# Two-layer decoder on one core: tokens loaded a second time in turned form, keys laid out by GpSimd, and a new written order

## The chip, the cores and the metric

The kernel runs on one core of a Trainium2 chip. The metric is device time in microseconds (us) of one execution, with all inputs in device memory at its start and the output there at its end. Before the change, three runs took 1685.7, 1693.88 and 1693.98 us; the median is 1693.88 us.

A core has these engines, each with an instruction queue of its own that is worked off in order: TensorE (PE: matrix products and transposes), VectorE (DVE), ScalarE (ACT), GpSimd (POOL) and SyncE (SP), which here only issues transfers (DMAs). Sixteen DMA engines move the data.

## The reference

What is computed, with 16 sequences of 256 tokens of 128 features, and 64 context rows of 96 features for each sequence:

```python
# layer 0
x = ln(x + attn0(x))                    # 16 heads of 8, causal, scale 1/sqrt(8)
x = ln(x + cross0(x, ctx))              # 8 heads of 16 over the 64 context rows
scores = softmax(x @ gate_w.T)
idx = top_k(scores + gate_b, 6)         # 64 experts, at most 64 tokens each
y = sum(scores[idx] * expert[idx](x))   # silu(x w1) * (x w3), then w2; 88 wide
z = (silu(x @ ws1.T) * (x @ ws3.T)) @ ws2.T
x = ln(x + y + z)
# layer 1
x = ln(x + attn1(x))                    # 16 heads of 64, causal
x = ln(x + cross1(x, ctx))              # 16 heads of 64 over the context rows
x = ln(x + ffn1(x))                     # layer norm, width-limited q, k, v, 8 heads of 16
```

The first attention of layer 0, whose beginning the change touches, computes q, k, v = x @ Wqkv.T, then dots = (q . k) * 8 ** -0.5 per head.

## The kernel before, in words

**Tiling.** A "batch" is one sequence: 256 tokens, which are two tiles of 128 partitions. The kernel goes through these phases:

- Layer 0 up to the routing, for batches 0 to 15: `layer0(b)`, lines 798 to 922. With it runs `contexts` (lines 768 to 782), work that belongs to layer 1: for eight pairs of heads it multiplies the context with the key and query weights (k1x, g1x) and with the value and output weights (v1x, h1x) and writes the products to device memory (gd, hd), from where layer 1 loads them. Each copy out of PSUM goes to a buffer of the tag "fold", of which there are four.
- Shared feed-forward (`shared`: sh, hs, z), groups 0 to 3 of 8.
- Experts, eight groups of eight (`expert_tokens` loads xe from xb, `expert_turned` transposes it, `expert_hidden`, `expert_out`).
- Shared feed-forward, groups 4 to 7.
- Layer 1, `layer1(b)`, lines 1099 to 1231, for batches 0 to 15. It begins by gathering the expert outputs of a batch (ge, from yb), adds them up on VectorE (xr), and goes on with layer norm, transposes and qk.

**One batch of layer 0.** The tokens x are loaded by SyncE (line 799) and transposed on TensorE into PSUM (tp_x), which VectorE copies to xT (`transposed`, lines 298 to 303). Two matmuls give queries and keys in one PSUM bank (qk). VectorE copies the queries and multiplies them by 8 ** -0.5 (qT, lines 809 to 810). The keys are laid out four times, each copy with other heads set to zero, so that four heads can be multiplied side by side on TensorE: `expanded` (lines 648 to 655) makes kx with two operations on VectorE and two on ScalarE, each of which multiplies by one column of the mask sm8. Scores s_0a, softmax (nm, p, ri, rx), transposes of the probabilities (ptp, pT), values (o_0a) and projection (pj_0a) follow, then the layer norm, whose power of -0.5 (rs) GpSimd computes. The residual with its bias (xpb) is also GpSimd's. The cross attention (names with 0x) has the same form; its keys kx0x are laid out by one GpSimd multiplication with broadcast operands.

Then comes the routing. The gate's logits (lg) are followed by a softmax on ScalarE and VectorE and the choice of six experts (chosen). The matmuls "pos" count how many tokens an expert already has; `run` holds the count of the batches before, and VectorE updates it with two additions (lines 890 to 892). From pos VectorE makes the slot numbers. For each of the 2 x 6 choices of a batch VectorE picks the weight (hit) and GpSimd issues an indirect DMA that writes 128 token rows into their slots in xb (192 scatters over the 16 batches). Each scatter waits for the "hit" of its own number. Slots that stay empty must be zero: `clear_slots` (lines 688 to 694) writes 4096 rows of 512 bytes of zeros into xb, and one row into yb, by SyncE's queue; it is recorded as the first part of `contexts`.

**What sets the order.** The instructions of layer 0 and of layer 1 are first recorded, not emitted: a `Recorder` keeps one list of units for each program (the contexts or one batch) and engine. `interleaved` then emits them in the order of a string, where one character stands for one program and one engine:

```python
    for c in order:
        b, e = divmod(LETTERS.index(c), len(ENGINES))
        for trace in waiting[b][e].pop(0):
            trace()
```

ORDER0 holds the order of layer 0 with the contexts, ORDER1 that of layer 1. Within `manual_schedule` the order on TensorE, VectorE, ScalarE and GpSimd stays as emitted; SyncE's transfers may be moved by the scheduler. There are four such stretches in the kernel before: layer 0, the experts, bv with l1_bout, and layer 1. Because the recorder's line 141 makes every call, all rows of the profile show L141, and operations are told apart by the names of their tiles.

**Start.** Loads go by SyncE in the order of the code: context, shared weights (ws1, ws3, ws2), then the weights of layer 0 (lines 656 to 676); the tokens of batch 0 follow in ORDER0. GpSimd builds the masks and sets vx0 and va0 to zero.

**Between experts and layer 1.** Two tiles vaf are set to zero by GpSimd (lines 1088 to 1089). bv is a broadcast copy on VectorE, eight matmuls multiply it with l1_wout (bv_out), and VectorE adds the result to l1_bout (lines 1091 to 1097). l1_bout is read by xpb_1a of batch 0. On VectorE the gathered sums (xr) of batch 0, as they were scheduled, lie between the last operations of the shared feed-forward (hs and the addition of z) and this copy.

## Time and profile before

| | |
|---|---|
| median of three runs | 1693.88 us |
| the profiled execution | 1679.19 us |
| its span (first to last instruction) | 1677.4 us |
| mean granted TensorE clock | 0.959 |
| TensorE busy | 1496.5 us (89%), 12738 matmuls |
| VectorE busy | 1244.2 us (74%), 3788 instructions |
| ScalarE busy | 1108.6 us (66%), 3811 instructions |
| GpSimd busy | 830.6 us (50%), 910 instructions |
| moved by DMA | 73.89 MB, 44 GB/s |
| layer 0, first pos of batch 0 / 8 / 15 | 86.4 / 364.1 / 602.0 us |
| first qk of layer 1 | 711.9 us |

The profile is one execution taken by the hardware profiler. A row of its groups of operations reads: line, engine, operation, names out<-in, shape out<-in, count, then the busy time in us and the mean of one in ns, then the idle time of the engine just before such rows and what ended that idle time. "Busy" does not say "bound": an engine can be busy beside the one that decides, and a stage of the kernel can be bound by another engine than the span as a whole. So shares are read stage by stage here. PEclk is the clock that TensorE was granted in a window, as a share of its full speed[...]. A row in order of time reads: start in us, duration in us, engine, line, operation, names, shapes; in square brackets stands the idle time of that engine before it and who ended it.

### The profile page before, as it was taken

How to read it: one execution, taken by the hardware profiler on the slowest of the kernel's cores; microseconds unless marked ns; L12 is line 12 of the kernel's file. 1: busy time of each engine (PE TensorE's matmuls, PEld its weight loads, DVE VectorE, ACT ScalarE, POOL GpSimd, SP SyncE). 2: the span in 40 equal slices, each digit the busy share in tenths (PEclk: the TensorE clock that was granted, in tenths of full speed). 3: DMA queues.
4: the chain of work that ended last, by engine and by line, in shares of the span. 5: the costliest groups of instructions: out<-in, count | busy, mean ns of one | idle time of the engine just before them, and what ended most of it. 6: DMA issues, size and time to landing. Idle time of an engine off the chain costs nothing.

```text
span 1677.4 us, 36931 instructions
## 1 busy us (share of the span) xinstructions
PE 1496.5 (89%) x12738; PEld 1080.5 (64%) x12738; DVE 1244.2 (74%) x3788; ACT 1108.6 (66%) x3811; POOL 830.6 (50%) x910
## 2 busy tenths in 40 slices
PE   7989988889987679688998999998999999999996
PEld 4655555556554338466776877686777677777774
DVE  5788888879887643355778878777786787788675
ACT  4776777757776312155576777677676767786766
POOL 2144445444435440456727656664564576564441
PEclk9999999989999778789999999999999999999999
DMA  4111111111100066474202233222322333220000
GB/s 142 60 41 34 60 32 33 42 48 55 47 13 1 1 172 190 52 105 48 23 14 34 40 41 44 23 36 14 48 41 31 30 43 42 36 23 4 5 1 11
DMA packets 117190, 73.89 MB, mean 44 GB/s; under 512 B 46555, under 2 KB 106808, under 8 KB 116877
## 3 DMA queue, kind: packets, MB, share of 16 engines
q1 hardware_dynamic: 104717, 58.55, 12.8%
q0 software_dynamic: 12288, 13.00, 10.6%
q8 instruction: 102, 1.67, 0.4%
q14 instruction: 83, 0.68, 0.1%
HBM read 48.05 MB, written 35.65 MB: 50 GB/s over the span
## 4 chain that ended last, share of the span: by engine, by line
PE 52%; DVE 24%; ACT 11%; issue 6%; POOL 4%; DMA 2%; another core or an unknown queue 1%; SPq 0%; POOLq 0%; DVEq 0%; ACTq 0%
PE s_1a L141 5%; PE qk L141 4%; PE o_1a L141 4%; ACT p_0a L141 4%; PE ptp_1a L141 3%; PE s_0a L141 3%; PE ptp_1f L141 3%; PE vp L141 3%; PE pj_1x L141 3%; PE pj_1a L141 2%; PE ptp_0a L141 2%; DVE nm_0a L141 2%; PE s_1x L141 2%; ACT p_1a L141 2%; DVE x L141 2%
## 5 line engine op out<-in xcount | busy, mean ns | idle before, releaser
L141 POOL DMA_INDIRECT xb<-x,slots x192 | 189.1, 985 | 263.9 <-DVE hit L141 212.6
L141 POOL TENSOR_TENSOR p_1a<-p_1a,ri_1a 128x512 f32<-128x512 f32 x192 | 197.3, 1039 | 104.5 <-DVE ri_1a L141 89.3
L141 ACT ACTIVATE p_1a<-s_1a,nm_1a 128x256 f32<-128x256 f32 (+1 forms) x512 | 210.9, 445 | 50.5 <-DVE nm_1a L141 41.7
L141 ACT ACTIVATE p_0a<-s_0a,nm_0a 128x256 f32<-128x256 f32 (+1 forms) x512 | 211.5, 451 | 35.2 <-DVE nm_0a L141 33.6
L141 POOL DMA_INDIRECT ge<-yb,slots x192 | 195.7, 1019 | 54.4 <-issue 51.9
L141 ACT COPY pT_1a<-ptp_1a 128x512 f32<-128x512 f32 x192 | 106.1, 618 | 63.1 <-PE ptp_1a L141 55.1
L141 DVE TENSOR_REDUCE nm_1a<-s_1a 128x2 f32<-128x512 f32 (+1 forms) x192 | 126.1, 673 | 21.4 <-PE s_1a L141 21.3
L141 DVE TENSOR_REDUCE nm_0a<-s_0a 128x2 f32<-128x512 f32 (+1 forms) x192 | 125.0, 682 | 11.8 <-PE s_0a L141 10.5
L141 PE MATMUL qk<-x3T,l_wqkv 128*128 128x256 f32 x512 | 126.9, 390 | 2.7 <-issue 1.4
L141 ACT ACTIVATE p_1f<-s_1f,nm_1f 128x256 f32<-128x256 f32 x256 | 119.0, 499 | 10.4 <-DVE nm_1f L141 9.3
L141 PE MATMUL ptp_0a<-ident,p_0a 128*128 128x128 f32 x768 | 112.1, 281 | 13.5 <-ACT p_0a L141 7.9
L141 ACT COPY pT_0a<-ptp_0a 128x512 f32<-128x512 f32 x192 | 106.4, 615 | 23.7 <-PE ptp_0a L141 18.6
L141 ACT ACTIVATION_READ_ACCUMULATOR p_0a<-s_0a,nm_0a 128x1 f32 x512 | 120.8, 236 | 0.0
L141 ACT ACTIVATION_READ_ACCUMULATOR p_1a<-s_1a,nm_1a 128x1 f32 x512 | 117.9, 230 | 0.0
L141 PEld LDWEIGHTS qk<-x3T,l_wqkv 128*128 128x128 f32 x512 | 95.8, 197 | 20.1 <-issue 7.7
L141 PEld LDWEIGHTS ptp_0a<-ident,p_0a 128*128 128x128 f32 x768 | 86.4, 143 | 34.0 <-ACT p_0a L141 20.6
L141 PE MATMUL ptp_1a<-ident,p_1a 128*128 128x128 f32 x768 | 101.1, 275 | 7.7 <-POOL p_1a L141 3.9
L141 PE MATMUL s_1a<-kT,qT 64*128 64x256 f32 (+1 forms) x1024 | 104.4, 342 | 3.3 <-issue 2.3
L141 POOL TENSOR_TENSOR p_1x<-p_1x,cri_1x 128x512 f32<-128x512 f32 x64 | 65.9, 1044 | 66.6 <-DVE cri_1x L141 41.9
L141 PE MATMUL o_1a<-pT_1a,v 128*64 128x128 f32 x1536 | 95.4, 276 | 3.0 <-ACT p_1a L141 1.2
L141 PEld LDWEIGHTS s_1a<-kT,qT 64*128 64x128 f32 x1024 | 81.5, 192 | 23.3 <-issue 11.4
L141 DVE SCALAR_TENSOR_TENSOR xr<-ge,slot_w,xr 128x128 f32<-128x128 f32 x160 | 61.2, 383 | 46.8 <-DMA ge<-yb,slots 42.7
(258 smaller groups left out, 3710.9 us busy)
## 6 DMA issues: line engine op xcount, KB each, us to landing
gd<-g1x_sb SPq DMA_DIRECT2D x32, 256.0 KB
hd<-h1x_sb SPq DMA_DIRECT2D x32, 256.0 KB
gx<-gd SPq DMA_DIRECT2D x16, 512.0 KB
hx<-hd SPq DMA_DIRECT2D x32, 256.0 KB
xb<-x,slots POOLq DMA_INDIRECT x192
ge<-yb,slots POOLq DMA_INDIRECT x192
e<-in_w1T SPq DMA_DIRECT2D x8, 352.0 KB
e<-in_w3T SPq DMA_DIRECT2D x8, 352.0 KB
```

The source lines that it names most:

```text
L141: r = f(*[made(x) for x in a], **{n: made(x) for n, x in k.items()})
```

## The change

- The tokens are handed over in a second, transposed copy in device memory (xT). `tokens(b)` loads both forms, with three buffers each; the two transposes on TensorE and VectorE's copy of a batch go away.
- At the start SyncE first issues the tokens of batch 0 and wqkv, then the context and the weights of the context keys and values, then the others; the shared weights come last.
- The zero fill of xb and yb is issued from ScalarE's queue, ahead of ScalarE's other work.
- The factor 8 ** -0.5 is multiplied once into the query columns of wqkv, on VectorE (128x128).
- Queries and keys leave PSUM in one ScalarE copy of 128x512 (qkT, two buffers). The four-fold layout of the keys, kx, is one GpSimd multiplication of 128x1024 with two broadcast operands.
- The two additions for `run` move from VectorE to GpSimd.
- vaf is set to zero by VectorE instead of GpSimd.
- There is one `manual_schedule` for all that follows the start. With it the VectorE order before layer 1 is that of the code: hs and z of the last shared groups, vaf, bv and l1_bout come ahead of all xr.
- ORDER0 is another string, with 2492 units instead of 2542. The matmuls of the contexts 1 to 7, which lay in the first 80% of layer 0's TensorE order, now lie in its last 61%; three and a half contexts come after pos of batch 13, and the last of them entirely after pos of batch 15, ahead of the shared feed-forward. ORDER1 keeps the order on TensorE and ScalarE; on VectorE some ten neighbours change places, on GpSimd one rs and two gathers, on SyncE two transfers.

```diff
@@ -32,66 +32,65 @@
 ORDER0 = (
-    ',\'#\'#$#$+$(#)($()*#*))$(*)*)()*))*())*)()*(*()*#*$#*#$**($**(#*)#$%(\'\'$%()\'\')(()*()*(1*)0-#.*((*-**.-(*..(*)#*'
...
+    '\'(16;(*#)+*)#*$#$+$()()*))*())*)()*(*()*#*$#*#$**($**(#*)#(())(()*$*(*$(()*)-*(*-*2.*((*)7**2*(3/40/4.3/74(80@'
...
 ORDER1 = (
...
@@ -654,25 +653,43 @@
-    ctxT = load("ctxT", [DC, B, KV], pool=xt_pool)
     fw = pool_of(phase_ab, name="fw", bufs=2)
-    ws1 = load("ws1T", [D, 2 * INTER], pool=xt_pool)
...
+        def tokens(b):
+
+            x = x0_pool.tile([P, 2, D], F32, tag="xin", bufs=3, name=f"x_{b}")
+            xT = x0_pool.tile([P, T], F32, tag="xinT", bufs=3, name=f"xT_{b}")
+            nc.sync.dma_start(xT, a["xT"][:, b * T : (b + 1) * T])
+            nc.sync.dma_start(x, a["x"][b * T : (b + 1) * T, :].rearrange("(i p) d -> p i d", p=P))
+            return x, xT
+
+        tokens0 = tokens(0)
         l0_wqkv = load("l0_wqkvT", [D, 3 * D], pool=x0_pool)
+
+        nc.scalar.dma_start(
+            xb.rearrange("(s p) d -> p s d", p=P),
+            zero.unsqueeze(1).to_broadcast([P, NSLOT // P, D]),
+        )
+        nc.scalar.dma_start(yb[NSLOT : NSLOT + 1, :], zero[0:1, :])
+
+        nc.vector.tensor_scalar(l0_wqkv[:, :D], l0_wqkv[:, :D], float(8**-0.5), None, ALU.mult)
+        ctxT = load("ctxT", [DC, B, KV], pool=xt_pool)
...
@@ -684,14 +701,6 @@
-        def clear_slots():
...
@@ -797,19 +805,18 @@
-            xT = w2.tile([P, T], F32, tag="xT", name=f"xT_{b}")
-            transposed(x, xT, f"x_{b}")
+            x, xT = tokens(b) if b else tokens0
...
-            qT = w2.tile([P, 1, T], F32, tag="qT0", name=f"qT0_{b}")
-            nc.vector.tensor_scalar(qT[:, 0, :], qk[:, :T], float(8**-0.5), None, ALU.mult)
+            qkT = x0_pool.tile([P, 2, T], F32, tag="qkT0", bufs=2, name=f"qkT0_{b}")
+            nc.scalar.copy(qkT.rearrange("p i t -> p (i t)"), qk)
             kx = kx_pool.tile([P, 4, T], F32, tag="kx0", name=f"kx0_{b}")
-            expanded(qk[:, T:], sm8, kx)
+            nc.gpsimd.tensor_tensor(
+                kx, qkT[:, 1, :].unsqueeze(1).to_broadcast([P, 4, T]), sm8.unsqueeze(2).to_broadcast([P, 4, T]), ALU.mult,
+            )
...
@@ -887,9 +894,9 @@
-            nc.vector.tensor_tensor(run, chosen[:, 0, :], chosen[:, 1, :], ALU.add)
+            nc.gpsimd.tensor_tensor(run, chosen[:, 0, :], chosen[:, 1, :], ALU.add)
             if run_before is not None:
-                nc.vector.tensor_tensor(run, run_before, run, ALU.add)
+                nc.gpsimd.tensor_tensor(run, run_before, run, ALU.add)
...
@@ -921,8 +928,8 @@
-        with tc.manual_schedule(engines=MANUAL):
-            interleaved(rec, [contexts] + [partial(layer0, b) for b in range(B)], ORDER0)
+        ctx.enter_context(tc.manual_schedule(engines=MANUAL))
+        interleaved(rec, [contexts] + [partial(layer0, b) for b in range(B)], ORDER0)
...
@@ -1086,15 +1092,14 @@
     for t in vaf:
-        nc.gpsimd.memset(t, 0.0)
+        nc.vector.memset(t, 0.0)
...
-    with tc.manual_schedule(engines=MANUAL):
-        nc.vector.tensor_copy(bv, l1_bqkv[:, 16:24].unsqueeze(2).to_broadcast([P, 8, P]))
...
+    nc.vector.tensor_copy(bv, l1_bqkv[:, 16:24].unsqueeze(2).to_broadcast([P, 8, P]))
...
@@ -1244,6 +1248,7 @@
         "x": g["x"].reshape(B * T, D),
+        "xT": g["x"].reshape(B * T, D).T,
```

## The prediction

> **What bounds the kernel now.** I read the chain that ended last, then busy time per stage, then the groups by shape, then single engines in order of time. The chain says which engine to watch:
>
> ```profile
> PE 52%; DVE 24%; ACT 11%; issue 6%; POOL 4%; DMA 2%; another core or an unknown queue 1%; SPq 0%; POOLq 0%; DVEq 0%; ACTq 0%
> ```
>
> Half of the span hangs on TensorE, a quarter on VectorE. The stages say where: window, its length, busy time (instructions) per engine, granted clock, DMA share.
>
> ```profile
> core 0: us, PE busy (x) PEld busy (x) DVE busy (x) ACT busy (x) POOL busy (x), PEclk, DMA share, GB/s
> 0.00:20.00 20.00, 12.80 (x66) 8.51 (x66) 7.85 (x28) 2.23 (x4) 9.47 (x30) 1.00 0.74 208
> ...
> 86.40:158.70 72.30, 64.46 (x549) 40.35 (x548) 61.16 (x220) 51.76 (x193) 34.00 (x37) 0.98 0.12 38
> ...
> 295.90:364.10 68.20, 58.54 (x539) 37.00 (x540) 56.69 (x207) 46.83 (x173) 30.76 (x33) 1.00 0.14 43
> ...
> 540.00:602.00 62.00, 33.27 (x245) 19.01 (x246) 40.08 (x164) 20.38 (x63) 26.03 (x28) 0.71 0.02 2
> ...
> 602.00:630.00 28.00, 25.62 (x103) 13.67 (x104) 11.79 (x51) 4.53 (x8) 14.57 (x15) 0.85 0.92 265
> ...
> 675.00:712.00 37.00, 24.24 (x107) 16.65 (x105) 13.30 (x32) 3.64 (x7) 18.12 (x20) 0.73 0.43 55
> ...
> 742.00:1677.00 935.00, 872.62 (x7638) 681.17 (x7636) 711.25 (x1940) 666.25 (x2214) 535.87 (x575) 0.98 0.23 29
> ```
>
> Layer 1 (742 to 1677) is 935 us long and TensorE is busy for 872.6 of them, 93%. The middle of layer 0 (two of its stretches shown) runs at 89% on TensorE and 85% on VectorE: nearly balanced. Two windows hold idle TensorE: the end of layer 0 (540 to 602, 33 of 62 us, clock 0.71) and the start of layer 1 (675 to 712, 24 of 37). I measure layer 0 by the first "pos" matmul of each batch: batch 0 at 86.4 us, batch 12 at 503.2, batch 15 at 602.0, about 35 us a batch.
>
> Prices from the groups by shape (busy sum, mean ns after the bar):
>
> ```profile
> L141 DVE TENSOR_SCALAR kx<-qk,sm 128x256 f32<-128x256 f32 x28 | 13.2, 476 | 2.9 <-ACT kx L141 2.5 <-issue 0.4
> ...
> L141 ACT ACTIVATE kx<-qk,sm 128x256 f32<-128x256 f32 x28 | 12.1, 481 | 13.5 <-DVE kx L141 8.6 <-PE qk L141 3.0 <-issue 1.8
> ...
> L141 POOL TENSOR_TENSOR kx0x<-kT0x,hm 128x512 f32<-128x512 f32 x13 | 13.6, 1048 | 0.0
> ```
>
> and from VectorE's order in time (start, duration):
>
> ```profile
> 303.41 0.41 DVE L141 COPY xT<-tp_x 128x256 f32<-128x256 f32 x1
> ...
> 307.04 0.42 DVE L141 TENSOR_SCALAR qT<-qk 128x256 f32<-128x256 f32 x1 [0.63 <-ACT kx L141]
> ...
> 324.48 0.18 DVE L141 TENSOR_TENSOR run<-chosen 128x64 bf16<-128x64 bf16 x1
> ...
> 301.35 0.23 DVE L141 COPY rx_0a<-ri_0a 128x128 f32<-128x128 f32 x1
> ...
> 332.19 1.37 DVE L141 COPY rx_0a<-ri_0a 128x128 f32<-128x128 f32 x1
> ```
>
> The last row is the same kind of copy as the one before it, but took 1.37 us instead of 0.23. GpSimd's row at that time is
>
> ```profile
> 332.43 1.04 POOL L141 TENSOR_TENSOR kx0x<-kT0x,hm 128x512 f32<-128x512 f32 x1
> ```
>
> so the copy ended with the GpSimd multiply. From 70 to 530 us, each VectorE operation that overlaps a GpSimd elementwise one, against the median of its kind: 66 such GpSimd operations, 52.7 us long, added 14.0 us to VectorE (27%), and the 13 kx0x rows (13.6 us) alone 5.6 (41%).
>
> **The change part by part.**
>
> *Tokens loaded turned, scale folded, one eviction, run on GpSimd.* Each batch loses on VectorE the copy xT (0.42), qT (0.42), two kx (0.95) and two run additions (0.37): 2.16 us, times 16 = 34.6 us. ScalarE loses two kx (0.96) and gains one 128x512 copy (0.61, as pT): 0.35 x 16, about 5 us less. TensorE loses the pair tp_x, 0.4 to 0.7 us, about 0.5 x 16 = 8 us. The second token load is 128 KB per batch while the DMA share is 0.12 to 0.14 and it is issued batches ahead: nothing; uncovered, one load of about 2 us a batch.
>
> *Keys on GpSimd.* No 128x1024 row exists. From 128x256 (0.74) to 128x512 (1.048) a straight line gives 1.66 us, doubling the latter gives 2.10; I take 2.08, as the kx0x row has the same two operands with a broadcast. That is 33 us of GpSimd in all, plus 31 run additions at 0.5 to 0.72 (128x2 and 128x256 rows are 0.72 and 0.74), near 19. GpSimd was busy 0.45 of the middle; 52 us more over 530 is 0.55, no bound by itself. But the Trainium skill ("SBUF — State Buffer", section "Who interferes with whom") speaks against the change: VectorE and GpSimd share a port pair under an exclusive lock, and a VectorE operation with two SBUF inputs or in a fast mode waits for the whole GpSimd instruction. Taken fully, 33 us of kx would stall VectorE for 33 us and eat the 34.6. The rows above say that only 27 to 41% of GpSimd time comes back as delay, because operations from PSUM and gaps fall under it too: 9 to 14 us for kx, 5 for run. I take 16; 14 to 40 goes into the range. VectorE nets 34.6 - 16 = 18.6 us less. On the latency of one batch: qk then went through 0.42 + 4 x 0.48 on two engines, now 0.61 + 2.08, about 1 us later; 27 to 83 TensorE rows lie between qk and the first s_0a in the new order (some 10 us), which cover it. Behind kx on GpSimd wait xpb, rs and scatters; ahead of it may stand a scatter that waits for "hit".
>
> *Zero fill and load order at the start.*
>
> ```profile
> 8.32 5.53 SPq L141 DMA_DIRECT2D yb<-zero  x1
> ...
> 19.94 1.14 PE L141 MATMUL s_0a<-kx,qT 32*128 32x512 f32 x8
> ```
>
> The 2 MB fill of xb sits on SyncE's queue and the first s_0a runs at 19.94 us. After, tokens and wqkv go first, and the fill goes to ScalarE's queue. Against a fill that is out of the way: the skill's page "DMA: Bandwidth & Descriptors", section "Issuing engines are not separate DMA queues", says that transfers issued from another engine share the same 16 DMA engines. The DMA share of the first 20 us, 0.74, and its 4096 rows of zero agree with a shared resource. By the order alone s_0a could come at 12; with shared engines, ScalarE's first copy behind the issue and GpSimd's masks (until about 9) ahead of kx, I estimate 16. Against these 4 us, 32 v0x matmuls, about 2 us of filler, come later. Net -2, between -6 and +3.
>
> *The new order of layer 0.* After removing 8 us, TensorE has 510 - 8 = 502 us up to the last pos; the order also puts the last context (67 us / 7 = 9.6 each) behind it, so 492. The other contexts move from the first 80% of layer 0 to 39 to 100% of it; 2.5 of them (24 us, less 5 for token work that moved too, so 19) now fill the end of layer 0. I build the time of the last pos: 16 us of start with 10 busy; an end window of 62 us now holding 33 + 19 = 52; and 492 - 10 - 52 = 430 between them at the same 0.893, 482 us. Sum 560, against 602: -42. By VectorE alone (478 - 18.6, same shares) it would be 548, so TensorE decides. If the middle falls to 0.87 from waits on GpSimd, +13; if the end only takes half of its filler, +8. The clock was at half for 7, 14 and 20 us of the end window; if a fuller TensorE avoids this, 10 more, kept for the range.
>
> *The last context ahead of the shared feed-forward.* It is 9.6 us of matmuls, but with four buffers for its evictions and its writes to memory. Between 602 and 630 TensorE was busy for 25.6 of 28 us, so nothing absorbs it: 10 to 19, I take +14. The gathers of expert tokens had to wait for the last scatter (620.2) and were done at 629.8; shifting with the end of layer 0 they stay covered. The expert weights' loads interleave with the context's writes; they wait for layer 0's buffers as before, 0.
>
> *Start of layer 1.*
>
> ```profile
> 699.96 0.80 PE L141 MATMUL z<-ws2T,hs 88*128 88x128 f32 x2 [7.14 <-DVE hs L141]
> ...
> 711.92 9.16 PE L141 MATMUL qk<-x3T,l_wqkv 128*128 128x256 f32 x32 [0.61 <-DVE x3T L141]
> ```
>
> ```profile
> 674.53 0.99 POOL L141 MEMSET vaf<- 128x512 f32 x2 [53.32 <-PE yp L141]
> ...
> 711.29 0.72 POOL L141 TENSOR_TENSOR xpb_1a<-x,l_bout 128x256 f32<-128x256 f32 x1 [5.02 <-DVE l_bout L141]
> ```
>
> z waits 7.14 us for hs, whose VectorE operations stood ready from about 688 but behind xr operations that waited for gathers; xpb_1a waits 5.02 for l_bout for the same reason. The change puts the last hs, bv and l_bout ahead of all xr and moves vaf's memsets (0.99 each) to VectorE, where they fall in idle time (13.3 busy of 37). With l_bout early, qk of layer 1 follows the gathers (last landed 698.3), rs (700.3), norm and transposes: about 705.3 instead of 711.9. -6, between -8 and 0. Uncovered, the memsets cost 2.
>
> *Experts and layer 1.* TensorE's order from the first shared matmul to the end is the same row by row; VectorE differs by neighbour swaps. 0, with ±2.
>
> Sum: -42 (which contains the -2 of the start) + 14 - 6 = -34. The profiled execution is 1679.2 us with a span of 1677.4; the after one should be about 1645 with a span of 1643. The median before is 1693.9, 15 us above it (lowest 1685.7); the same difference on the median gives 1660.
>
> **The rivals.** What counts as a difference is 0.5%, 8.5 us.
>
> *The gain is half eaten.* GpSimd delays VectorE by its full time (the skill's rule), 40 against 34.6: no gain there. Left are half of TensorE's 8, the filled end (-19), the start (-2), layer 1 (-6), the context (+14): -17, 1677. For it: the 1.37 us copy. Against: only 41% in sum.
>
> *No change.* The contexts only move: in the end window they lengthen it by the 19 they save earlier, as VectorE holds 40 of its 62 us, and the last costs 19 against 9.6 saved. Then -8 - 6 - 2 + 9 = -7, 1687. For it: VectorE is the busiest there. Against: TensorE stands half of that window.
>
> *Slower.* GpSimd is one in-order queue. In the middle its scatters waited for "hit" for 184 us in 71 waits, 2.6 us each and up to 11. If the order puts kx behind such a scatter, kx arrives late, s_0a after it, and TensorE stands, as this is the head of a batch's attention. With 34 us of gain over 16 batches the break-even is 2.1 us per batch on the path; slower by over 0.5% from 2.7. One mean wait plus kx uncovered, 2.6 + 2.08, would be 75 us: +41, 1735; 3.1 a batch gives 1710. For it: the new wait crosses three engines, before two. Against: those 10 us of TensorE rows between qk and s_0a.
>
> **How the numbers follow.** The likeliest case, -20 to -55, gets 0.52; half eaten (-8.5 to -20) 0.18; no change (within 8.5) 0.08; slower 0.22. So faster 0.70, same 0.08, slower 0.22. The likeliest case's own range is 1639 to 1674. Up through the two middle cases to the first part of the slower one, and down by the clock (-10) and VectorE's sum (-12): 1634 to 1704 leaves out 0.05 below and 0.13 above.
>
> **What would show it.** Right: the last pos near 560; a share above 0.89 for TensorE in the middle and about 0.84 in the last 60 us before that pos, with a clock near 1; GpSimd's kx rows near 2.1 us; the first expert-token transposes some 40 us after the last pos instead of 28; from the last shared matmuls to qk of layer 1 about 6 us less; 935 us of layer 1 unchanged. Wrong: s_0a waiting for kx in the chain of waits; VectorE delayed by more than 20 us in sum; kx rows much over 2.1; the middle at or above 35 us a batch; the context's rows behind the last pos spread over more than 19 us.

## The result: 1.1% slower, and the profile after

The changed kernel takes 1710.2 us (median; lowest 1706.95, highest 1714.88), against 1693.9 us before: a ratio of 1.011, interval 1.007 to 1.015. The forecast was 1660 us, 34 us less; it came out 16 us more.

The profiled execution after the change took 1714.9 us, with a span of 1712.8 us and a mean granted TensorE clock of 0.951 (0.959 before). Between the two profiled executions lie 35 us, more than between the medians: the one of before (1679.2 us) was quicker than each of its timed runs (1685.7 us and more), and the one of after was the slowest of its four. The shares of the chain that ended last hardly moved:

```profile
PE 51%; DVE 24%; ACT 10%; issue 6%; POOL 4%; DMA 3%; another core or an unknown queue 3%; SPq 0%; POOLq 0%; DVEq 0%; ACTq 0%
```

"Another core or an unknown queue" went from 1% to 3%, with one core running; the last section comes back to this. Next the windows of the changed kernel (us, busy time and instructions per engine, granted clock, DMA share), cut at the same events as those of before: start, two stretches of two batches each (from the first pos of batch 0 and of batch 6), the end of layer 0 (from the first pos of batch 12), the time behind the last pos, the start of layer 1 and the rest.

```profile
core 0: us, PE busy (x) PEld busy (x) DVE busy (x) ACT busy (x) POOL busy (x), PEclk, DMA share, GB/s
0.00:20.00 20.00, 10.64 (x56) 5.75 (x56) 7.83 (x24) 5.00 (x20) 10.60 (x30) 1.00 0.73 210
...
85.70:156.40 70.70, 57.40 (x515) 36.56 (x515) 52.74 (x194) 50.13 (x195) 32.90 (x38) 0.95 0.03 8
...
296.20:369.50 73.30, 63.08 (x558) 40.22 (x557) 59.54 (x206) 53.10 (x193) 39.98 (x44) 0.98 0.16 48
...
516.10:613.40 97.30, 77.49 (x619) 45.62 (x618) 70.01 (x266) 50.16 (x166) 41.56 (x47) 0.89 0.19 61
613.40:645.00 31.60, 22.43 (x91) 10.04 (x90) 12.50 (x46) 8.26 (x14) 14.51 (x17) 0.89 0.82 250
...
700.00:737.00 37.00, 22.93 (x109) 15.60 (x108) 15.28 (x35) 3.64 (x7) 17.22 (x18) 0.76 0.73 109
...
767.00:1712.80 945.80, 878.96 (x7636) 683.25 (x7634) 711.60 (x1938) 667.74 (x2213) 535.52 (x574) 0.98 0.24 28
```

In the stretch from 85.7 TensorE is busy for 57.4 of 70.7 us (81%) and VectorE for 52.7 (75%); before, the same stretch had 89% and 85% (64.46 and 61.16 of 72.3). The work is gone from both engines, and the stretch is only 1.6 us shorter. In the end window TensorE is busy for 77.5 of 97.3 us: the filler is where the new order puts it and the clock is 0.89, and still the window is only 1.5 us shorter than the same three batches before (503.2 to 602.0), with batch 11 ahead of it 14 us longer (45.0 instead of 31.0).

Where the 35 us between the two spans lie, by events of the two traces (us; differences from unrounded times):

| | before | after | difference |
|---|---|---|---|
| first s_0a | 19.9 | 15.1 | |
| first pos of batch 0 | 86.4 | 85.7 | -0.8 |
| first pos of batch 0 to that of batch 11 | 385.8 | 385.5 | -0.3 |
| first pos of batch 11 to that of batch 15 | 129.8 | 142.3 | +12.5 |
| last pos to first expert tokens on TensorE (xet) | 27.8 | 42.2 | +14.4 |
| xet to the first gather (ge) | 48.6 | 47.8 | -0.8 |
| first gather to the first s_1a | 46.1 | 46.6 | +0.6 |
| first s_1a to the end | 953.0 | 962.8 | +9.8 |

Rows two to eight add up to the 35.4 us. The last row is, for the most part, no effect of the change: on one chip a kernel with the layer 1 of before (nofold_before, below) took 960.2 us for it and the changed kernel 960.7. What remains is a loss of 12 us in the last four batches, one of 14 us behind them, and, in eleven batches, no gain at all.

### The profile page after: what moved, and what is told of

Same layout as the page of the kernel before. It is cut to its first block, busy times and chain, and to the rows that moved or that the text cites. A ratio compares the mean times of both kernels' runs of the same rounds, so it can differ in the third digit from the quotient of the medians.

```text
span 1712.8 us, 36846 instructions
## 1 busy us (share of the span) xinstructions
PE 1507.9 (88%) x12706; PEld 1087.0 (63%) x12706; DVE 1226.5 (72%) x3696; ACT 1106.2 (65%) x3795; POOL 870.0 (51%) x955
## 4 chain that ended last, share of the span: by engine, by line
PE 51%; DVE 24%; ACT 10%; issue 6%; POOL 4%; DMA 3%; another core or an unknown queue 3%; SPq 0%; POOLq 0%; DVEq 0%; ACTq 0%
PE s_1a L140 5%; PE qk L140 4%; PE s_0a L140 4%; PE ptp_1a L140 3%; PE o_1a L140 3%; ACT p_0a L140 3%; PE ptp_0a L140 3%; DVE nm_0a L140 3%; PE pj_1x L140 3%; PE pj_1a L140 2%; PE ptp_1f L140 2%; PE vp L140 2%; DMA ge<-yb,slots 2%; PE s_1x L140 2%
## 5 line engine op out<-in xcount | busy, mean ns | idle before, releaser
L140 ACT COPY pT_0a<-ptp_0a 128x512 f32<-128x512 f32 x192 | 108.3, 617 | 37.1 <-PE ptp_0a L140 30.4
L140 PE MATMUL ptp_0a<-ident,p_0a 128*128 128x128 f32 x768 | 117.0, 291 | 17.0 <-ACT p_0a L140 5.9
L140 PEld LDWEIGHTS ptp_0a<-ident,p_0a 128*128 128x128 f32 x768 | 92.0, 149 | 39.2 <-ACT p_0a L140 12.9
L140 PEld LDWEIGHTS ptp_1a<-ident,p_1a 128*128 128x128 f32 x768 | 87.9, 143 | 16.1 <-POOL p_1a L140 8.6
```

The source lines that it names most:

```text
L140: r = f(*[made(x) for x in a], **{n: made(x) for n, x in k.items()})
```

## The experiments

My theory after the result was that the new places of the contexts' work (k1x, g1x, v1x, h1x; "folds" from here on) had spent what the edits saved. The rival was that the edits had saved nothing. The experiments ran in six sets, each on one chip and beside the kernel before, and the chips differ: before took 1654.1 us in set 1, 1694.2 in set 2, 1653.1 in set 3 (on the chip of set 1), 1681.9 in set 4, 1691.9 in set 5 and 1682.2 in set 6. The chips have the numbers 12 (sets 1 and 3), 3, 0, 9 and 5; that of the result is not known ("first" below). Ratios are always to before on the same chip, with a 95% interval in brackets; places in time come from one profiled execution of each kernel.

### Set 1: order and edits taken apart

All edits, but layer 0 in the written order of before; e3_new_end is the reverse, layer 0 of before and everything behind it as changed.

```diff
 # eA_edits_old_order, against after
 ORDER0 = (
-    '\'(16;(*#)+*)#*$#$+$()()*))*())*)()*(*()*#*$#*#$**($**(#*#)(())(()*$*(*$(()*)-*(*-*2.*((*)7**2*(3/40/4.3/74(80@'
+    "#'#$#$$#($(*++#)$(*)*)()*))*())*)()*(*()*#*$#*#$**($**(#*)#$%(''$%()'')(()*()*(1*)#*((*-**/00-(*.(*)#***(/%.(*-/"
...
 # e3_new_end, against before
+    ctx.enter_context(tc.manual_schedule(engines=MANUAL))
...
-        nc.gpsimd.memset(t, 0.0)
+        nc.vector.memset(t, 0.0)
...
```

> All edits of the change (turned tokens, scale in the weights, one ScalarE eviction, keys and run on GpSimd, zero fill on ScalarE's queue, new loads, new start of layer 1), but layer 0 in the order of before: its units keep their places, the context folds lie in the first 78% again, and only the units that an edit removes or adds are taken out or put in. If the new order is what costs (theory ORDER), this is faster than before by 10 to 35 us, about 1660 to 1680, with the last pos before 600 us. If the operations themselves cost, above all keys on GpSimd (theory POOL), it is slower than before by 10 us or more, near the changed kernel's 1710.

> The kernel before up to the end of layer 0, the changed kernel from the experts on: one scope, bv, l1_bout and the zeros of vaf ahead of the gathered sums on VectorE, the new order of layer 1. By the prediction's step, 6 us less than before (-8 to 0). By the rival reading of the changed kernel's trace, the gathered sums now wait for bv_out and l_bout and the gain is given back: within 2 us of before. If layer 1 in the new order is itself slower (its stretch was 10 us longer in the profile), 8 to 12 us more.

Two more move the folds alone: e1_ctx_early puts those of the changed kernel at the shares of TensorE's order where before has them, e2_before_ctx_late puts those of before where the changed kernel has them.

```diff
 # e1_ctx_early, against after
 ORDER0 = (
-    '\'(16;(*#)+*)#*$#$+$()()*))*())*)()*(*()*#*$#*#$**($**(#*#)(())(()*$*(*$(()*)-*(*-*2.*((*)7**2*(3/40/4.3/74(80@'
+    "'(16;(*#)+*)#*$#$+$()()*))*())*)()*(*()*#*$#*#$**($**(#*#)(())(()*$#*(*$($'%'#()*)-$'%'#*(*-%*2.*((#*)7**2%*(3/4"
...
 # e2_before_ctx_late, against before
 ORDER0 = (
-    ',\'#\'#$#$+$(#)($()*#*))$(*)*)()*))*())*)()*(*()*#*$#*#$**($**(#*)#$%(\'\'$%()\'\')(()*()*(1*)0-#.*((*-**.-(*..(*)#*'
+    ",'#'#$#$+$(#)($()*#*))$(*)*)()*))*())*)()*(*()*#*$#*#$**($**(*)(())(()*()*(1*)0-.*((*-**.-(*..(*)***(///.(*-/).("
...
```

> The changed kernel with the eight context folds moved back to the share of layer 0 where before had them (2% to 78%); the order of the sixteen batches among themselves stays the new one. ORDER by the folds' place: the 19 us of the last fold ahead of the shared feed-forward go, TensorE fills its gaps in the middle and keeps its clock; 15 to 40 us less than the changed kernel, 1670 to 1695. If folds in the middle cost their own TensorE time there (67 us spread over the first 13 batches, +20 or more), it gains nothing: 1700 to 1715. POOL: no change but for the last fold, about 1690.

> The kernel before with nothing changed but the place of the eight folds: they lie in the last 58% of layer 0, four and more of them behind the batch 13, the last behind the last pos, as in the changed kernel. ORDER by the folds' place: slower than before by 10 to 25 us (1700 to 1715), with a granted clock below 0.95 in the first half. If the place of the folds is no cause: within 8 us of before.

Measured, on chip 12: eA 0.9974 (0.9953 to 0.9994), e3 1.0028 (1.0012 to 1.0044), e1 1.022 (1.0171 to 1.0269), e2 1.032 (1.0271 to 1.0369). So the edits of layer 0 save 0.5% (1649.2 against 1657.9 us), and the last pos goes from 596.2 (e3) to 588.9 us (eA): -7.3 us. The forecast's sum holds 8 us of TensorE for these edits, 9 us at its share of 0.893 (its 18.6 us of VectorE were the looser bound and not in the sum), so on this chip the edits by themselves came out near their size. The windows of eA:

```profile
core 0: us, PE busy (x) PEld busy (x) DVE busy (x) ACT busy (x) POOL busy (x), PEclk, DMA share, GB/s
89.40:157.00 67.60, 59.39 (x532) 36.97 (x529) 55.81 (x200) 49.71 (x188) 36.16 (x38) 1.00 0.13 39
...
431.00:500.00 69.00, 57.97 (x552) 37.95 (x550) 58.12 (x217) 53.98 (x201) 39.06 (x43) 1.00 0.10 32
```

VectorE is busy for 83 to 84% here, no engine is full, and a batch (half of a row) takes 34 us. Moving the folds to places that were not written for them costs 2 to 3%, in either direction. e2 holds a second lesson: up to its first pos of batch 5 it has run 8 of the folds' 384 matmuls, where e3, with before's folds, has run 192, and that pos is at 261.6 us in e2 and at 261.5 in e3. Folds at the places of before cost nothing that this shows.

### Set 2: the folds' matmuls removed, and the keys back

nofold_before and nofold_after leave out every matmul of the folds (k1x, g1x, v1x, h1x); their evictions read a tile of zeros and the writes to memory stay. e4_keys_back makes kx with the four operations on VectorE and ScalarE again, now from qkT.

```diff
 # nofold_before and nofold_after
-                nc.tensor.matmul(
-                    t, w, ctxT[:, g * 8 : (g + 1) * 8, :].rearrange("p b k -> p (b k)"),
-                    start=True, stop=True,
-                )
...
-                move(k, t)
+                move(k.rearrange("p (i d) -> p i d", d=P), zeros)
...
 # e4_keys_back, against after
-            nc.gpsimd.tensor_tensor(
-                kx, qkT[:, 1, :].unsqueeze(1).to_broadcast([P, 4, T]), sm8.unsqueeze(2).to_broadcast([P, 4, T]), ALU.mult,
-            )
+            expanded(qkT[:, 1, :], sm8, kx)
```

> The changed kernel as it is, on the chip of the runs below, as their measure: slower than before by 0.7 to 1.5%, as at first.

> The kernel before without the matmuls of the eight folds: their evictions (from a tile of zeros), stores and loads stay where they were, so the weights that layer 1 reads are zeros. If the folds fill waits of TensorE that are there anyway (theory GAPS: a batch's pace is set by the chain of its softmax rounds, not by TensorE's load), the time falls by less than 15 us of the 67 that the matmuls take. If TensorE's load sets the pace, as the prediction's division by 0.893 assumed (theory LOAD), by 55 to 75 us.

> The changed kernel without the matmuls of the folds, in the same manner. GAPS: the folds lie late, where there is no room for them, so much more is saved than in the kernel before: 30 to 60 us against the changed kernel, which would then be level with or faster than the kernel before without folds. LOAD: the same 55 to 75 us in both, so that the difference of the two kernels stays.

> The changed kernel with the keys laid out by VectorE and ScalarE again, two operations each, out of the same copy, at the place of the GpSimd operation. POOL (the rival on record: keys late on GpSimd, or VectorE locked out by it): 15 us or more faster than the changed kernel. If GpSimd's keys are no cause: within 5 us of the changed kernel, or slower by up to 15 as VectorE gets 15 us back.

Measured: after_again (the changed kernel unedited) 1.0095 (1.0066 to 1.0123), nofold_before 0.9985 (0.9969 to 1.0), nofold_after 1.0067 (1.0028 to 1.0107), e4 1.0092 (1.0061 to 1.0122).

nofold_before is the run that decides. It takes 67 us of matmuls out of layer 0 of the kernel before, and the time changes by 0.15%, its first pos of batch 15 from 602.0 (profile of before) to 601.1 us. Its windows:

```profile
core 0: us, PE busy (x) PEld busy (x) DVE busy (x) ACT busy (x) POOL busy (x), PEclk, DMA share, GB/s
...
86.00:158.00 72.00, 56.11 (x479) 35.04 (x480) 58.32 (x204) 49.06 (x183) 33.92 (x37) 0.88 0.10 30
...
296.00:364.00 68.00, 52.19 (x458) 34.40 (x459) 55.04 (x206) 46.84 (x173) 30.93 (x33) 0.88 0.13 38
...
503.00:602.00 99.00, 64.22 (x506) 38.84 (x507) 68.67 (x272) 47.66 (x168) 44.51 (x48) 0.79 0.02 3
```

The window from 296 had TensorE busy for 58.5 us at clock 1.00 before, and now 52.2 us at 0.88; both take 68 us. Part of the room came back as a lower granted clock (the whole span: 0.939 instead of 0.959): up to 602 us, TensorE's matmuls other than the folds' kept it busy for 443.9 us before and for 461.5 here, so 17.6 of the 67 us were spent again. Nothing of the rest became time. The Trainium skill ("TensorE: Matmul & The Clock Gate", section "What's actually happening") has a gate that lowers the clock according to how busy the array has been, and these rows agree. What the run shows is the net of two effects, less work and a slower clock. As an estimate from these numbers, if all of the 17.6 us lay on the path of the batches, as much would have been gained by less work and lost again by the clock; the share of 0.893 asks for 75 us (67 / 0.893). So most of TensorE's load was not what the batches waited for; whether its speed was a part of it stays open.

In the changed kernel the matmuls are worth 0.3%, within the intervals of the two runs. And by the medians of e4 it is all the same, within 0.3%, which engine lays out the keys. Its trace says more: with VectorE and ScalarE doing that work again, the last pos is at 604.3 us instead of 612.1 (after_again, on the same chip; the five traces of the changed kernel have 611.6 to 614.6). So in the new order the keys on GpSimd cost layer 0 some 8 us. Part of this is gone at the end (the spans are 3.6 us apart), and the medians, 2.1 us apart, do not resolve what is left.

### Set 3: the folds wholly removed

noall_before and noall_after leave out the folds' matmuls, evictions, writes and the loads of their weights; layer 1 loads the same amount of data from two of its weight inputs instead. e6 has all edits of layer 0, in the old order, and the code of before from the experts on.

```diff
 # noall_after, against after (noall_before likewise, against before)
-            for c in range(8):
-                w = {}
...
-                fold_outputs(c, vT, w["wo"])
...
-        nc.sync.dma_start(gx, gd[:, :, b * KV : (b + 1) * KV].rearrange("h p k -> p h k"))
+        nc.sync.dma_start(gx, a["l1_wqkv"][:, 64 * b : 64 * b + 1024].rearrange("p (h k) -> p h k", k=KV))
...
 # e6_edits_old_order_old_end, against eA_edits_old_order
-        ctx.enter_context(tc.manual_schedule(engines=MANUAL))
-        interleaved(rec, [contexts] + [partial(layer0, b) for b in range(B)], ORDER0)
+        with tc.manual_schedule(engines=MANUAL):
+            interleaved(rec, [contexts] + [partial(layer0, b) for b in range(B)], ORDER0)
...
```

> The kernel before without the folds as a whole: no matmuls, evictions, stores and loads of theirs; layer 1 loads the same amount from other inputs in place of the folds. Theory FREE (the folds of the old order lie in waits of all engines and of the queues): less than 10 us below before. If their evictions and stores cost in the old order too: 15 to 30 us below.

> The changed kernel without the folds as a whole, in the same manner. Theory TAIL (the loss of the changed kernel is what the late folds do to VectorE, ScalarE, the four fold buffers and SyncE's queue behind batch 11, not their matmuls): 25 to 40 us below the changed kernel, so 10 to 20 us below the kernel before, with pos(11) to pos(15) at 120 to 126 us instead of 142 and the first expert transposes 28 us behind the last pos instead of 41. If the rest of the new order is what costs: it stays within 10 us of the changed kernel, and pos(11) to pos(15) stays at 142.

> All edits up to the end of layer 0 in the order of before, and from the experts on the code and order of before (zeros of vaf on GpSimd again). From the two runs on one chip (0.9974 with the new end, 1.0028 for the new end alone) it should be 0.5% faster than before, 5 to 12 us; if the new end was not the cause of the 1.0028, 0.2 to 0.3%.

Measured, on chip 12: noall_before 0.9958 (0.9943 to 0.9973), noall_after 0.9853 (0.9829 to 0.9876), e6 0.999 (0.9972 to 1.0008). Without any fold, then, edits and new order together are worth 1.05%, and 18 us in layer 0: the last pos is at 594.0 in noall_before and at 575.9 in noall_after. These 18 us are not to be held against the forecast's 42, of which some 32 (19 + 9.6 us at the share of 0.893) were to come from moving the folds: without folds its sum leaves 13 (9 for the edits, 4 for the start). So the rest of the change does help on this chip, by more than was forecast. It also says that the folds cost 7 us at the places of before, and it moved my suspicion to where the changed kernel has them. (e6 keeps the end of before and is no faster than eA, so the new end isn't what keeps eA from gaining more.)

### Set 4: the folds placed anew

In e7 the folds of the changed kernel are spread evenly over layer 0 (starting at shares 0.05 to 0.90 of TensorE's order), at places chosen one by one by when their buffers and engines come free.

```diff
 # e7_folds_fitted, against after
 ORDER0 = (
-    '\'(16;(*#)+*)#*$#$+$()()*))*())*)()*(*()*#*$#*#$**($**(#*#)(())(()*$*(*$(()*)-*(*-*2.*((*)7**2*(3/40/4.3/74(80@'
+    "'(16;(*#)+*)#*$#$+$()()*))*())*)()*(*()*#*$#*#$**($**(*)(())(()**(*(()*)-*(*-*2.*((*)7**2*(3/40/4.3/74(80@*-)5.("
...
```

> The changed kernel with the order of its sixteen batches kept and only the folds' units placed anew: evenly over the first 95% of layer 0's TensorE order, each at a place where the engines have a wait for it, its evictions some places behind. If the place of the folds is the whole loss, it is 8 to 30 us faster than the changed kernel and 0 to 15 us faster than before, with the last pos near 590 on a chip where before has 596 to 602. If folds cost in the new order wherever they lie, as the run with the folds at the old shares suggested, it stays at or above the changed kernel.

> The changed kernel once more, on the chip of the run above, as its measure; and, if it is a chip where before takes about 1654 us instead of 1694, to see how much of the loss is there too: by the traces of the other chips, in which all engines stand together for 10 to 14 us of layer 0, about half of the 17 us; if the loss is in the order alone, the same 1%.

Measured, on chip 0: e7 1.014 (1.0119 to 1.0161), the changed kernel beside it 1.0072 (1.005 to 1.0093). This even spreading is worse than the late bunch; my placing didn't repair it.

### Sets 5 and 6: which part of a fold, and which part of the change

nostore_after keeps the folds' matmuls and evictions and leaves out their writes (layer 1 loads from weights as above). noall_after_2 is noall_after on another chip, after_fourth the changed kernel beside them. On the last chip the edits in the old order (eA_again) run beside the changed kernel (after_fifth).

```diff
 # nostore_after, against after
-                    nc.sync.dma_start(gd[2 * c + r, :, g * 512 : (g + 1) * 512], k)
...
-                    nc.sync.dma_start(
-                        hd[2 * c + r, g * 512 : (g + 1) * 512, :].rearrange("(i p) d -> p i d", p=P),
-                        k.rearrange("p (i d) -> p i d", d=D),
-                    )
...
```

> The changed kernel as the measure of the two runs below on the same chip: 0.7 to 1.1% slower than before; on a chip of the quicker kind (before near 1654) 0 to 1.1%.

> The changed kernel with the folds' matmuls and evictions, but without their stores to memory (layer 1 loads as much from other inputs). If the late stores are what costs, by holding the four fold buffers and SyncE's queue ahead of the expert tokens, 15 to 35 us below the changed kernel; if the evictions on VectorE and ScalarE cost, within 8 us of it.

> The changed kernel without the folds as a whole, beside the changed kernel on one chip. From the ratios of two chips (1.0095 and 0.9853) it should be 2.4% or 41 us below the changed kernel; if a part of that was the chip, 15 to 30 us.

> All edits in the old order of layer 0, once more. On a chip where before takes about 1690 us: if the edits themselves are what meets the unexplained waits of those chips, slower than before by 5 us or more; if the new order meets them, 0.2 to 0.8% faster than before, as on the chip where before takes 1654.

> The changed kernel beside it. On a chip where before takes about 1654 us: 0.5% faster to 0.5% slower than before, if half of the loss of 1% is the unexplained waits, and 1% slower if not; on a chip where before takes about 1690, 0.7 to 1.1% slower as in four calls before.

Measured, on chip 9: after_fourth 1.0066 (1.0047 to 1.0085), nostore_after 1.0091 (1.0062 to 1.0119), noall_after_2 0.9991 (0.9968 to 1.0013). The writes aren't what the folds cost. All of the folds cost the changed kernel 0.75% here, against 0.42% for those of before on chip 12. But noall_after_2 should have stood near 0.985 as in set 3 if the folds had been the whole story. On chip 9 the changed kernel without any fold is no faster than before with all of them.

On chip 5: eA_again 1.0036 (1.0008 to 1.0064), after_fifth 1.007 (1.0046 to 1.0093). So of the 0.7% on this chip about half comes with the edits, which had gained 0.26% on chip 12, and half with the new order. Of the three versions that ran on more than one chip (the changed kernel, the edits in the old order, and noall_after), none is faster than the kernel before on all of them.

The pace of layer 0 in all of these, by the first pos of batches 0, 11 and 15 (us):

| kernel | chip | batch 0 to 11 | batch 11 to 15 | at batch 15 |
|---|---|---|---|---|
| before | first | 385.8 | 129.8 | 602.0 |
| before's layer 0 (e3) | 12 | 384.0 | 125.8 | 596.2 |
| nofold_before | 3 | 389.5 | 129.0 | 601.1 |
| noall_before | 12 | 382.4 | 125.8 | 594.0 |
| edits, old order (eA) | 12 | 376.3 | 123.2 | 588.9 |
| edits, old order (eA_again) | 5 | 387.5 | 128.6 | 605.5 |
| changed (after) | first | 385.5 | 142.3 | 613.4 |
| changed (after_again) | 3 | 382.3 | 144.0 | 612.1 |
| changed, keys back (e4) | 3 | 378.5 | 142.4 | 604.3 |
| changed (after_fifth) | 5 | 386.4 | 141.5 | 611.6 |
| nofold_after | 3 | 386.3 | 142.7 | 614.3 |
| noall_after | 12 | 372.0 | 121.4 | 575.9 |
| noall_after_2 | 9 | 383.8 | 135.9 | 604.3 |

Two things stand out. The last four batches of the changed kernel take 141 to 144 us with the matmuls of the folds or without them, 136 (chip 9) or 121 (chip 12) when their evictions are gone too. And a program that ran on chip 12 and on another is 17 (eA) or 28 us (noall_after) later there at the last pos.

## Why the prediction was wrong

**The step that failed** is "430 between them at the same 0.893, 482 us". It took a busy share for a constant: remove work from TensorE, divide what is left by the same share, and the time must shrink. nofold_before removed 67 us of it and the share fell instead; the batches kept their pace. Of the forecast's 42 us, some 32 hung on that division alone: the 19 us of contexts moved into the end window and the 9.6 of the last one, at 0.893. The forecast's own cut of the time up to the last pos shows it (before, then after; columns as in the windows above):

```profile
20.00:540.00 520.00, 463.69 (x4061) 290.56 (x4059) 430.14 (x1506) 388.74 (x1458) 210.31 (x228) 0.98 0.14 41
```

```profile
16.00:551.40 535.40, 453.94 (x3859) 286.80 (x3855) 401.17 (x1397) 371.05 (x1409) 245.41 (x267) 0.93 0.10 30
551.40:613.40 62.00, 50.30 (x396) 30.10 (x394) 48.15 (x190) 28.75 (x85) 29.73 (x35) 0.92 0.27 85
```

The end window is as forecast: 50.3 us busy of 62 (the sum had 52). The middle is not: 453.9 us busy in 535.4, a share of 0.848, where the sum had 430 in 482. 202 matmuls fewer than before saved TensorE 9.8 us of busy time, as the granted clock went from 0.98 to 0.93, and the middle is 15.4 us longer. "By VectorE alone", my cross-check, used the same division and shared the error: VectorE is busy for 401.2 us of that middle instead of 430.1, and the middle did not shrink with it.

What sets the pace instead is, I think, the latency of a batch's rounds (scores, maximum, exponent, transposes, values, each on another engine) through four queues in a fixed order. For it: a batch takes 34 to 36 us with 77 to 89% on TensorE and 75 to 85% on VectorE alike (before, after, eA and nofold_before), with neither full. I counted from the code that all eight PSUM banks are in use at the peak of both written orders, which may keep a round from starting early; no run varied the number of banks. This part is argued, not shown, and how much of it is TensorE's clock is open, as said above.

Point by point:

- *Start: s_0a at 16.* 15.1; right. But the first pos of batch 0 came only 0.8 us earlier (predicted: 2 net). The gain was gone within the batch.
- *VectorE 34.6 less, 16 given back.* The first half is right as busy time: the rows that went away took 36.0 us in the trace of before, and VectorE's busy time up to the last pos fell from 478.1 to 453.3 us. Between 70 and 530 us the VectorE operations that overlap GpSimd's elementwise ones were delayed by 22.5 us in all (14.0 before), 27% of GpSimd's 84.4 us, so 8.5 more, not 16. But the two kernels differ in order too. In one order and on one chip, the 52 kinds of VectorE rows that layer 0 of after_again and of e4 share are together 13.9 us longer in after_again, which has the 30.4 us of kx on GpSimd (46%): inside the 9 to 14 us that the forecast gave to kx. The rule that I weighed (the Trainium skill, "SBUF — State Buffer", section "Who interferes with whom": a blocked operation waits for the whole GpSimd instruction) would have made it over 30 if taken for every operation; the rows of before had the better number. As time, eA against e3 gave 7.3 us of layer 0 on chip 12.
- *Keys on GpSimd at 2.08, run at 0.5 to 0.72.* The groups of the changed kernel on GpSimd between 86 and 470 us (busy sum, mean ns, idle before):

```profile
L140 POOL TENSOR_TENSOR kx<-qkT,sm 128x1024 f32<-128x1024 f32 x10 | 19.0, 1903 | 3.4 <-ACT qkT L140 3.2
...
L140 POOL TENSOR_TENSOR run<-run,run 128x64 bf16<-128x64 bf16 x10 | 3.2, 316 | 0.8
L140 POOL TENSOR_TENSOR run<-chosen 128x64 bf16<-128x64 bf16 x10 | 3.0, 303 | 12.3 <-DVE chosen L140 12.3
```

  1.90 us and 0.30 to 0.32: kx a bit cheaper, run about half. The 3.4 us in the kx row are only waits for qkT. By GpSimd's order in time, six of the 16 kx rows did stand behind scatters, and began 1.6 to 5.2 us after qkT was ready; but the idle time in front of these scatters is 4.5 us in all, and only one s_0a waited for kx, for 0.25 us (at 43.55). So the rival on the slower side, whose 1710 us for 3.1 us a batch is the measured time, hit it by luck: its wait on the path isn't there. e4, with the keys off GpSimd at 1.0092 beside 1.0095, rules the keys out as the whole loss, not as the 8 us of layer 0 named above.
- *Contexts as filler: "2.5 of them now fill the end of layer 0".* They did (77.5 of 97.3 us busy, clock 0.89), but the last four batches got 12.5 us longer, and the eleven batches they left got 0.3 us shorter. The rival "no change" said just this, except that it let the contexts save as much earlier as they cost later. They saved nothing earlier, because they had cost nearly nothing there: 0.15% for the matmuls on chip 3, 0.42% for all of a fold on chip 12. What they cost at the end is not their matmuls (nofold_after: 142.7 us for the last four batches), and by the nostore run not their writes; with evictions gone as well it is 135.9 us on chip 9. I take it to be the evictions, which sit on VectorE's and ScalarE's queues between the rounds; no run removed them alone, so this isn't shown.
- *The last context ahead of the shared feed-forward: +14, and 40 us from the last pos to the expert tokens.* 14.4 and 42.2; right. The first shared matmul comes 19.0 us behind the last pos (I had 10 to 19), as TensorE waits between the last fold's products (5.28 us ahead of g1x, 1.38 and 0.65 ahead of h1x), and the shared work up to the expert tokens then takes 23.3 instead of 27.6 us, since it starts at the full clock. The first row of it before, and after:

```profile
602.21 1.99 PE L141 MATMUL sh<-x2T,ws1T 128*88 128x512 f32 x2
```

```profile
632.36 1.09 PE L140 MATMUL sh<-x2T,ws1T 128*88 128x512 f32 x2
```

  "Shifting with the end of layer 0 they stay covered" held for the gathers by little. In nofold_after the shared work starts right behind the last pos (614.6), and then TensorE waits for the load xe:

```profile
650.96 2.02 PE L139 MATMUL xet<-ident,xe 128*128 128x128 f32 x8 [5.12 <-DMA xe<-xb]
```

  There, and in the changed kernel, xe stands on SyncE's queue behind the last fold's writes and the weight loads after them. Before, SyncE reached xe 5.8 us after GpSimd's last scatter into xb (620.24 to 626.01), in the trace of after_again 14.5 us (631.70 to 646.23), and there the queue reads

```profile
635.78 2.17 SPq L140 DMA_DIRECT2D hd<-h1x_sb  x4
...
639.95 4.45 SPq L140 DMA_DIRECT2D f_qwT<-in_f_qwT  x1
...
646.23 4.55 SPq L140 DMA_DIRECT2D xe<-xb  x5
```

  In nostore_after xe is issued 4.2 us after the last scatter, and the expert tokens still come 42.6 us behind the last pos: with the fold's matmuls in place, TensorE's own order is the longer path. So two paths end there within some 5 us of each other (the tokens 36.7 us behind the last pos in nofold_after, 41.3 in after_again), and taking one away gives no more than that.
- *Start of layer 1: -6.* +0.6. The wait that I named is gone: z waited 7.14 us for hs before, and now

```profile
715.78 1.83 PE L140 MATMUL z<-ws2T,hs 88*128 88x128 f32 x14 [0.28 <-DVE hs L140]
...
723.80 3.75 PE L140 MATMUL bv_out<-l_wout,bv 128*128 128x128 f32 x16 [6.19 <-DVE bv L140]
```

  VectorE's order now has bv and l_bout ahead of all twelve xr, and l_bout waits for the matmuls of bv_out, a step that I had left out (VectorE in order of time):

```profile
720.74 1.29 DVE L140 TENSOR_TENSOR x<-z,x 128x512 f32<-128x512 f32 x2 [5.01 <-remote]
...
723.02 0.63 DVE L140 COPY bv<-l_bqkvT 128x1024 f32<-128x1024 f32 x1
727.59 0.29 DVE L140 TENSOR_TENSOR l_bout<-l_bout,bv_out 128x128 f32<-128x128 f32 x1 [3.94 <-PE bv_out L140]
727.79 0.35 DVE L140 SCALAR_TENSOR_TENSOR xr<-ge,slot_w,x 128x128 f32<-128x128 f32 x1
...
735.31 0.42 DVE L140 COPY x3T<-tp_x 128x256 f32<-128x256 f32 x1 [0.57 <-PE tp_x L140]
```

  The sums that before were done one by one as the gathers landed (681.2 to 698.4, the first gather at 678.4) all start at 727.8 now, 24.4 us after the first gather (703.4). That alone doesn't eat the gain. On chip 12, with the same VectorE order, first gather to first s_1a took 40.4 us in e3, 40.7 in eA and 40.8 in e1 (44.0 in noall_after), against 46.0 to 46.1 in the three traces there with the end of before: about the forecast's -6. The difference is the first row above. The last z was done at 717.61, and its addition began 3.1 us later, after a wait that nothing on this core ended; in e3 z was done at 691.31 and the addition follows at once:

```profile
691.34 0.69 DVE L140 TENSOR_TENSOR x<-z,x 128x512 f32<-128x512 f32 x1 [1.09 <-PE z L140]
```

  All eleven traces with the new end on other chips have this wait (2.4 to 3.6 us behind z, ended by "remote"), the four on chip 12 do not; behind it bv_out takes 3.75 us in the changed kernel and 2.03 in e3. It is of the kind that the last section shows. Still, nothing came of the -6 in e3's time either: its gathers began later (52.8 us behind the expert tokens on TensorE, where the three traces with the end of before have 45.1 to 49.1), for a reason that isn't known.
- *Experts and layer 1: 0, with ±2.* On chip 3 right: 960.7 in after_again, 960.2 in nofold_before. On chip 12 the new layer 1 took 936.5 to 941.2 us in four traces and the old one 934.4 to 934.7 in three, so there it is 2 to 7 us slower, which agrees with e3's 1.0028; no run took that apart.

In sum: -42 became +11.4, the context +14 became +14.4, and layer 1's start -6 became +0.6. Most of layer 1's own +9.8 lies between two executions (960.2 and 960.7 us on chip 3), and without it the traces differ by 26 us. The medians differ by 16; the rest I can't place, since the profile of before was that kernel's quickest execution.

## What to carry to other kernels

A high busy share of an engine isn't a bound: before dividing what is left by the share, take out a block of its work that nothing else waits for, and see whether the stage gets shorter, with the granted clock beside it. In a kernel with a written order, work moved into idle time brings its evictions, buffers and queued transfers along, and in these runs they cost more at a place not worked out for them than the matmuls did anywhere. When a wait is removed by moving an instruction ahead, follow what stands behind that instruction for one step more, on every queue, SyncE's too, and test the explanation on a run in which the same order did bring the gain; and compare kernels on one chip, then on a second.

## What the runs showed of the hardware

**One program, different chips.** I hadn't expected 40 us (2.4%) between chips for the kernel before: 1653 to 1654 us on chip 12, 1682 to 1694 on the others, each repeated over its set of runs. And the kernels aren't slowed alike: the last pos of noall_after is at 575.9 us on chip 12 and at 604.3 on chip 9. ScalarE's groups of both runs between 86 and 560 us, first on chip 12:

```profile
L138 ACT COPY rT_0x<-rtp_0x 128x128 f32<-128x128 f32 x28 | 8.3, 296 | 7.1 <-PE rtp_0x L138 7.1
L138 ACT COPY rT_0a<-rtp_0a 128x128 f32<-128x128 f32 x28 | 8.1, 290 | 14.7 <-PE rtp_0a L138 14.6
```

and on chip 9:

```profile
L138 ACT COPY rT_0x<-rtp_0x 128x128 f32<-128x128 f32 x26 | 7.7, 298 | 11.1 <-remote 7.3 <-PE rtp_0x L138 3.5 <-PE ptp_0a L138 0.3
L138 ACT COPY rT_0a<-rtp_0a 128x128 f32<-128x128 f32 x27 | 7.3, 270 | 27.9 <-PE rtp_0a L138 16.2 <-remote 5.0 <-PE ptp_0a L138 3.9
```

The operations are as long, but on chip 9 there are waits that end with nothing that the trace knows on this core ("remote"). One of them in the changed kernel (after_again, chip 3, all engines):

```profile
110.92 0.33 PE L140 MATMUL rtp_0x<-ident,rx_0x 128*128 128x128 f32 x1
...
113.27 0.27 ACT L140 COPY rT_0x<-rtp_0x 128x128 f32<-128x128 f32 x1 [3.73 <-remote]
...
113.59 0.66 PE L140 MATMUL ptp_0a<-ident,p_0a 128*128 128x128 f32 x4 [2.23 <-ACT rT_0x L140]
```

The product rtp_0x was done at 111.25, its copy began at 113.27, and TensorE waited for the copy. Such waits stand at the same instructions in run after run of the changed kernel on chips 3, 0, 9 and 5 and the first one, and at none on chip 12; in the old order layer 0 has one of over 1.5 us in before and none in nofold_before. Stretches of more than 0.6 us in layer 0 in which TensorE, VectorE and ScalarE all stand still sum to 0 us in before, 11.9 in after, 2.4 in eA_again and 13.4 in noall_after_2, but 1.5 in eA and 1.1 in noall_after, both on chip 12. So the new order meets these waits more often than the old one; standing still alone covers 12 of the 28 us between the two runs of noall_after. The remainder isn't spread evenly either: matched operation by operation, VectorE of eA_again falls behind that of eA in steps of 1 to 2.4 us at single operations. What they are stays open: the loads of instructions in the trace showed no fixed relation to them, and the changed kernel itself was not timed on chip 12. A comparison on one chip would have given this change either sign for its edits: -0.26% or +0.36%.

**Part of the room given to TensorE came back as clock.** 67 us less of matmuls, and the granted clock of the span fell from 0.959 to 0.939 in the old order and from 0.951 to 0.926 in the new.
